# First-layer edits in a two-layer decoder kernel: rotary tables, gate silus, a rotation in PSUM, weight centring

## The chip, the cores and the metric

The kernel runs on one core of a Trainium2 chip. The core has five engines that work side by side, each on its own queue of instructions in a fixed order: PE (TensorE, matmuls and transposes), DVE (VectorE), ACT (ScalarE, activation functions), POOL (GpSimd) and SP (SyncE, which here only starts transfers). Data lies in SBUF (on-chip memory of 128 partitions) and in PSUM (eight banks of 128 x 512 floats, which matmuls write). An engine waits at an instruction until the semaphores of what it needs are set. The metric is device time in microseconds (us), the median of several executions.

## The reference

Two decoder layers work on x of 4 batches x 256 tokens x 256 columns, all in float32. Each layer adds three terms:

```python
x = x + attn(layernorm(x))
x = x + mamba(ctx_1024, layernorm(x))
x = x + ffn(layernorm(x))
```

The first attention has 8 query heads and 2 key heads of 32 columns, a window of 64 tokens, tanh-capped scores and a normalisation behind the rotation. The second has 16 query heads and 4 key heads of 128 columns, with a layer norm of each head ahead of the rotation:

```python
q = _layernorm(q, qn_g, qn_b)
k = _layernorm(k, kn_g, kn_b)
q = q * cos + _rotate_half(q) * sin
k = k * cos + _rotate_half(k) * sin
```

The middle term is a state-space scan over the tokens of ctx_1024, gated by the normalised x:

```python
state = state * dA + (d * u)[..., None] * b[:, None, :]
y = jnp.einsum('bdn,bn->bd', state, c)
...
y = y + D[None, :, None] * x
y = y * silu(z)
```

Here z is the layer norm of the decoder's x. The first feed-forward is a gated one of 704 columns, the second a mixture of 32 experts with a shared one.

## The kernel before

The code is written with a tile framework: it is traced in program order, and the framework then fixes each engine's order itself from its own estimate of times, with code that stands earlier preferred, and sets all waits. A tile of a pool and a tag takes one of that tag's `bufs` buffers. So an engine's order in the trace isn't the order of the code: code that stands far behind fills gaps where its inputs are ready.

The program order is this. `conv_taps(0)` and `mamba_front(0, 0)` prepare the scan of batches 0 and 1 (`s00`). For each batch b, `head0(b)` projects, rotates and normalises queries, keys and values, and `tail0(b)` does scores, softmax, values and output; between them some steps of a scan are run. `head0` works in two halves of 128 tokens (c): the projection `pq` is in the only bank of pool `pa`; L359 multiplies 320 columns by the cosines into `r`, L360 the halves-swapped columns by the sines into `rr`, L365 (ACT) copies the values, and once both halves are there, L368 adds `rr` to `r`. The scan of batches 2 and 3 (`s01`) begins during batch 0.

A scan state (one of 16 per channel half) is an exponential on ACT (L215), a product on POOL (L217), the scan itself on DVE (L218), a product with C on DVE (L220), and a sum: on PE into a bank (L235) for even states, on POOL into y (L237) for odd ones; L239 adds the bank to y at the end of a half.

Behind the first attention, the constants and rows of the second layer (`cst1`, `row`) are asked for on ACT's queue (L513, L514). Then the weights of the second attention are centred, so that each head's projected vector has mean zero: one reduction over all 20 heads (L518), a scaling (L519), and one subtraction on POOL for each of two row blocks (L521).

The first feed-forward runs over two halves of two batches (`hf`). For each batch, `mamba_gate` takes layer-norm statistics of x (`ln_stats`: L120 and L121 on DVE, four small POOL steps L124 to L127), makes `sz` = silu of the normalised x on ACT (L252, two buffers), multiplies y by it (L256), transposes the product (L258) and adds it to x (L264); `ln_transposed` then takes statistics again, normalises (L136), transposes (L140) and copies the result out (L143). Both use the single bank of pool `pc`. Then the matmuls L551, the silu of the gate L559, the product L562 and the down-projection L575, which L583 adds to x. In the second half, `run(s01)` stands ahead of the gates: all that is left of that scan.

Then the pools of the first layer are closed and those of the second attention (`a1w`, `a1`, and eight PSUM banks anew) opened in their room. Seven POOL instructions for queries and seven for keys make the rotary tables (`cg`, `sg`, `bt`, L608 to L617) from `cst1` and `row`. Two transposes of the first `bt` (L626) give `btT` (L627). `keys_values(0)` follows: layer norm, projection (L640), squares (L655, ACT), rotation with the tables (L660 to L668, the product with `cg` in place in PSUM), scaling (L632, L633, L693). The second layer's scan, the attention and the experts (L941 to L955) fill the rest.

Of the kernel before, what the change touches and what calls it, by code (L numbers as in the profile page):

```python
# [10 lines left out]
F32 = mybir.dt.float32  # L11
BF16 = mybir.dt.bfloat16
I32 = mybir.dt.int32
AF = mybir.ActivationFunctionType
# [3 lines left out]
P = 128  # L18
# [23 lines left out]
def decoder_kernel(  # L42
# [203 lines left out]
    def mamba_gate(l, b, pool):  # L246

        nb, rs = ln_stats([x[:, 2 * b + c, :] for c in range(2)])
        pt = ps(pool)
        for c in range(2):  # L250
            sz = work.tile([P, S], F32, tag="sz", name="sz")
            nc.scalar.activation(  # L252
                sz, x[:, 2 * b + c, :], AF.Silu, bias=nb[:, c : c + 1], scale=rs[:, c : c + 1]
            )
            yg = work.tile([P, S], F32, tag="yg", name="yg")
            nc.vector.tensor_mul(yg, y_of[l, b // 2][:, c, (b % 2) * S : (b % 2 + 1) * S], sz)  # L256
            for lh in range(2):
                nc.tensor.transpose(  # L258
                    pt[:, lh * 256 + c * P : lh * 256 + (c + 1) * P],
                    yg[:, lh * P : (lh + 1) * P],  # L260
                    ident,
                )
        xb = x[:, 2 * b : 2 * b + 2, :]
        nc.vector.tensor_add(xb, xb, pt.rearrange("p (t d) -> p t d", t=2))  # L264
# [47 lines left out]
    with ExitStack() as ph:  # L312
# [27 lines left out]
        def head0(b):  # L340
# [5 lines left out]
            for c in range(2):  # L346
# [12 lines left out]
                nc.vector.tensor_mul(r[:, c, 0:10, :], q3, cos.unsqueeze(1).to_broadcast([P, 10, 32]))  # L359
# [4 lines left out]
                )  # L364
                nc.scalar.copy(  # L365
                    r[:, c, 10:12, :], pq[:, 320:384].rearrange("p (h d) -> p h d", d=32)
                )
            nc.vector.tensor_add(r[:, :, 0:10, :], r[:, :, 0:10, :], rr)  # L368
# [146 lines left out]

    wh = wqkv1[:, :, 0 : 20 * D1].rearrange("p f (h d) -> p f h d", d=D1)
    wmean = cpool.tile([P, 2, 20], F32, name="wmean")
    nc.vector.tensor_reduce(wmean, wh, AX.X, ALU.add)  # L518
    nc.vector.tensor_scalar(wmean, wmean, 1.0 / D1, None, ALU.mult)  # L519
    for f in range(2):  # L520
        nc.gpsimd.tensor_sub(wh[:, f], wh[:, f], wmean[:, f, :].unsqueeze(2).to_broadcast([P, 20, D1]))  # L521

    with ExitStack() as ph:
# [14 lines left out]
        for hf in range(2):  # L538
            if hf == 1:
                run(s01)  # L540
            xnT = wp.tile([P, 2, 512], F32, tag="f_xnT", name="f_xnT")
            for bb in range(2):
                mamba_gate(0, 2 * hf + bb, pc)
# [45 lines left out]
    with ExitStack() as ph:  # L589
# [7 lines left out]

        tabs = []
        for gcol, bcol in ((R_QG, R_QB), (R_KG, R_KB)):
            g_ = row[:, gcol - R_BR : gcol - R_BR + D1]  # L600
            b_ = row[:, bcol - R_BR : bcol - R_BR + D1]
            cg = wp.tile([P, 2, D1], F32, name=f"cg{gcol}")
            sg = wp.tile([P, 2, D1], F32, name=f"sg{gcol}")
            bt = wp.tile([P, 2, D1], F32, name=f"bt{gcol}")
            bs = wp.tile([P, 2, D1], F32, name=f"bs{gcol}")
            cos = cst1[:, 0:256].rearrange("p (c d) -> p c d", c=2)
            sin = cst1[:, C_SIN1 - C_COS1 : C_SIN1 - C_COS1 + 256].rearrange("p (c d) -> p c d", c=2)
            nc.gpsimd.tensor_mul(cg, cos, g_.unsqueeze(1).to_broadcast([P, 2, D1]))  # L608
            nc.gpsimd.tensor_mul(bt, cos, b_.unsqueeze(1).to_broadcast([P, 2, D1]))
            for lo, hi in ((0, 64), (64, 0)):  # L610
                for dst, v in ((sg, g_), (bs, b_)):
                    nc.gpsimd.tensor_mul(
                        dst[:, :, lo : lo + 64],
                        sin[:, :, lo : lo + 64],
                        v[:, hi : hi + 64].unsqueeze(1).to_broadcast([P, 2, 64]),
                    )
            nc.gpsimd.tensor_add(bt, bt, bs)  # L617
            tabs.append((cg, sg, bt))
# [535 lines left out]
```

## Time and profile before

| what | value |
|---|---|
| runs | 927.5, 925.39, 924.55 us; median 925.39 |
| profiled execution | 922.39 us, of which the span of instructions is 920.6 |
| mean granted PE clock | 0.931 |
| busy PE / DVE / ACT / POOL | 830.1 / 587.9 / 481.1 / 421.3 us (90, 64, 52, 46%) |
| chain that ended last, by engine | PE 42%, DVE 13%, ACT 7%, POOL 5%, issue 3% |
| first layer (0 to 324 us) | two scans, attention, feed-forward |
| second attention and its scan | 324 to 670 us |
| experts, first and second half | from 673 us to the end |

The page's second part cuts the span into 40 slices of 23 us; each digit is the busy share in tenths, PEclk the granted clock in tenths:

```profile
PE   4999899998978969789988979997999999999997
DVE  3697968666875549879678965867346676312221
ACT  2647635467949626757775765677624343211111
POOL 3263767657774643756673754233337761000000
PEclk9978758897997989999989999998999999999999
```

The first 14 slices are the first layer. No engine is full in all of them, and the clock falls in some of them below full. In the last six slices POOL has nothing, DVE and ACT little, and PE is full. The chain of waits and the timelines of this part are shown with the prediction.

### The profile page before, as it was taken

To read this page: it belongs to the slowest core of one execution; us is meant where nothing else is said; L and a number is where in the kernel's file an instruction comes from. 1 tells how busy PE (TensorE), PEld (TensorE's weight loads), DVE (VectorE), ACT (ScalarE), POOL (GpSimd) and SP (SyncE) were. 2 spreads that over 40 slices of the span, in tenths; PEclk is the share of its full clock that TensorE was granted. 3 is DMA by queue.
4 is the path that set the end of the run, shared out by engine and by line. 5 is a ranking of instruction groups with operands and counts; after the bars stand their busy time and mean duration, and the time that the engine had idled before them with its cause. 6 is when DMAs were issued, how large, how long until landed. Compare 5 with 4: busy or idle time off the path is not lost.

```text
span 920.6 us, 10256 instructions
## 1 busy us (share of the span) xinstructions
PE 830.1 (90%) x3074; PEld 517.2 (56%) x3074; DVE 587.9 (64%) x1096; ACT 481.1 (52%) x1187; POOL 421.3 (46%) x421
## 2 busy tenths in 40 slices
PE   4999899998978969789988979997999999999997
PEld 2455566643443425555664656674666666666665
DVE  3697968666875549879678965867346676312221
ACT  2647635467949626757775765677624343211111
POOL 3263767657774643756673754233337761000000
PEclk9978758897997989999989999998999999999999
DMA  4364436654541220111010200000137743554542
GB/s 158 101 188 168 140 119 183 202 183 165 179 166 51 68 92 1 58 35 46 24 68 6 79 33 23 24 1 2 48 92 234 232 152 102 163 149 146 160 152 80
DMA packets 60999, 98.36 MB, mean 107 GB/s; under 512 B 6336, under 2 KB 26704, under 8 KB 60688
## 3 DMA queue, kind: packets, MB, share of 16 engines
q1 hardware_dynamic: 59232, 95.77, 32.8%
q10 hardware_dynamic: 1712, 1.94, 0.7%
q8 instruction: 24, 0.39, 0.2%
q14 instruction: 31, 0.25, 0.1%
HBM read 96.24 MB, written 1.44 MB: 106 GB/s over the span
## 4 chain that ended last, share of the span: by engine, by line
PE 42%; DVE 13%; ACT 7%; POOL 5%; issue 3%; DMA 0%; SPq 0%; POOLq 0%; ACTq 0%; DVEq 0%
PE ps L941 12%; PE ps L955 12%; PE ps L809 5%; PE ps L640 3%; PE ps L747 2%; PE ps L794 2%; DVE h L218 2%; DVE ps L667 2%; ACT sc L766 2%; DVE qs L660 1%; DVE qr L668 1%; PE ps L674 1%; ACT L215 1%; POOL sc L771 1%; DVE hc L220 1%
## 5 line engine op out<-in xcount | busy, mean ns | idle before, releaser
L217 POOL TENSOR_TENSOR db<-bt,du 128x512 f32<-128x512 f32 x128 | 162.1, 1277 | 100.2 <-DVE h L218 67.9
L218 DVE TENSOR_TENSOR_SCAN h<-h,db 128x512 f32<-128x512 f32 x128 | 152.7, 1217 | 23.4 <-ACT h L215 22.0
L941 PE MATMUL ps<-moe_xnT,w 128*128 128x512 f32 x272 | 129.3, 598 | 0.0
L955 PE MATMUL ps<-w,hT 128*128 128x256 f32 x544 | 128.5, 379 | 0.0
L955 PEld LDWEIGHTS ps<-w,hT 128*128 128x128 f32 x544 | 103.0, 190 | 40.2 <-issue 29.4
L946 DVE SCALAR_TENSOR_TENSOR hT<-ps,gr 128x512 f32<-128x512 f32 x64 | 44.1, 689 | 127.0 <-PE ps L941 127.0
L215 ACT ACTIVATE h<-dt,negA 128x512 f32<-128x512 f32 x128 | 86.4, 689 | 59.2 <-DVE hc L220 58.5
L947 ACT ACTIVATE hT<-hT 128x512 f32<-128x512 f32 x68 | 42.8, 629 | 133.7 <-DVE hT L946 133.6
L640 PE MATMUL ps<-wqkv,xnT 128*128 128x512 f32 x192 | 94.8, 606 | 8.0 <-DVE rq L632 5.7
L220 DVE TENSOR_TENSOR hc<-h,ct 128x512 f32<-128x512 f32 x128 | 85.2, 679 | 3.4 <-DMA ct<-bc 0.9
L227 POOL TENSOR_TENSOR y<-y,hc 128x512 f32<-128x512 f32 x64 | 80.7, 1270 | 8.8 <-DVE hc L220 8.6
L633 POOL TENSOR_TENSOR rq<-rq,nhalf 128x8 f32<-128x8 f32 x20 | 32.9, 1647 | 90.2 <-DVE rq L632 90.0
L941 PEld LDWEIGHTS ps<-moe_xnT,w 128*128 128x128 f32 x272 | 51.7, 191 | 36.5 <-issue 33.2
L655 ACT ACTIVATE sq<-ps 128x128 f32<-128x128 f32 x160 | 42.3, 281 | 40.7 <-PE ps L640 37.5
L766 ACT ACTIVATE sc<-sc,nm 128x256 f32<-128x256 f32 (+1 forms) x128 | 56.7, 448 | 12.6 <-DVE nm L761 8.6
L771 POOL TENSOR_TENSOR sc<-sc,rsum 128x512 f32<-128x512 f32 (+1 forms) x32 | 46.2, 1466 | 34.5 <-DVE rsum L769 33.6
L809 PE MATMUL ps<-wo,oT 128*128 128x256 f32 x256 | 57.0, 381 | 0.4 <-ACT oT L802 0.4
L809 PEld LDWEIGHTS ps<-wo,oT 128*128 128x128 f32 x256 | 48.1, 190 | 9.2 <-ACT oT L802 2.6
L640 PEld LDWEIGHTS ps<-wqkv,xnT 128*128 128x128 f32 x192 | 33.5, 194 | 30.1 <-issue 17.7
L674 PE MATMUL ps<-ident,qr 128*128 128x128 f32 x160 | 28.4, 295 | 19.6 <-DVE qr L668 17.6
L235 PE MATMUL ps<-hc,ident 128*128 128x512 f32 x64 | 39.8, 712 | 5.5 <-DVE hc L220 5.3
L237 POOL TENSOR_TENSOR y<-y,hc 128x512 f32<-128x512 f32 x32 | 41.1, 1283 | 7.3 <-DVE hc L220 5.0
(205 smaller groups left out, 1505.5 us busy)
## 6 DMA issues: line engine op xcount, KB each, us to landing
bt<-bc SPq DMA_DIRECT2D x96, 256.0 KB, 3.6
ct<-bc SPq DMA_DIRECT2D x96, 256.0 KB, 3.7
w<-in_w_dram SPq DMA_DIRECT2D x64, 256.0 KB, 3.5
gr<-gt SPq DMA_DIRECT2D x64, 256.0 KB, 3.5
wqkv<-in_wqkv_dram SPq DMA_DIRECT2D x1, 3072.0 KB
wo<-in_wo_dram SPq DMA_DIRECT2D x1, 2048.0 KB, 8.6
x<-in_x_dram SPq DMA_DIRECT2D x4, 256.0 KB, 5.1
w<-in_ws_dram SPq DMA_DIRECT2D x4, 256.0 KB, 3.3
```

What stands on the lines that cost most here:

```text
L215: nc.scalar.activation(h, dt[:, c, :], AF.Exp, scale=negA[:, a : a + 1])
L217: nc.gpsimd.tensor_mul(db, bt, du[:, c, :])
L218: nc.vector.tensor_tensor_scan(h, h, db, 0.0, ALU.mult, ALU.add)
L220: nc.vector.tensor_mul(hc, h, ct)
L227: nc.gpsimd.tensor_add(y[:, c, :], y[:, c, :], state(n, c, bt, ct))
L640: mm(pq, lhsT=xnT[:, f, c * P : (c + 1) * P], rhs=wqkv1[:, f, ch * 512 : (ch + 1) * 512], start=(f == 0), stop=(f == 1),)
L766: nc.scalar.activation(part, part, AF.Exp, bias=nm[:, qc, j : j + 1], accum_out=rsum[:, qc, j : j + 1])
L771: nc.gpsimd.tensor_mul(part, part, rsum[:, qc, :].unsqueeze(2).to_broadcast([P, 4, w]))
L809: mm(pout[:, c * 256 : (c + 1) * 256], lhsT=oTs[h // 4][:, h % 4, c * P : (c + 1) * P], rhs=wo1[:, 8 * gp + h, :], start=(h == 0), stop=(h ...
L941: mm(ph_, lhsT=w[:, f * P : (f + 1) * P], rhs=xnT[:, f, :], start=(f == 0), stop=(f == 1))
L946: gated.append(nc.vector.scalar_tensor_tensor(h, ph_, 0.0, g, ALU.max, ALU.mult).ins)
L955: mm(po[t // 2][:, (t % 2) * 256 : (t % 2 + 1) * 256], lhsT=h[:, t * P : (t + 1) * P], rhs=w[:, 256:512], start=start and t % 2 == 0, stop ...
```

## The change

Four edits, all in the first layer's part of the program.

- The rotary tables of the second attention are made ahead of the weight centring, in a pool that lives through the whole kernel; the buffer `bs` is shared by both tables.
- A new function `gates_of` holds a gate's statistics and its two silus; `mamba_gate` takes its result, or calls it. In the first layer the gates of both batches of a half are asked for at the top of the half, in four buffers, for the second half ahead of `run(s01)`. In the second layer the gate is as before, save that both silus stand ahead of the first product.
- In `head0` the sines' product comes first, the cosines' product is written back to PSUM in place, and the sum is made for each half of 128 tokens, from PSUM and `rr`.
- The weight centring is cut into four pieces of five heads.

```diff
--- before.py
+++ after.py
@@ -243,17 +243,24 @@
             if next(gen, "end") == "end":
                 break
 
-    def mamba_gate(l, b, pool):
+    def gates_of(b, pool, bufs):
 
         nb, rs = ln_stats([x[:, 2 * b + c, :] for c in range(2)])
+        szs = []
+        for c in range(2):
+            szs.append(pool.tile([P, S], F32, tag="sz", name="sz", bufs=bufs))
+            nc.scalar.activation(
+                szs[c], x[:, 2 * b + c, :], AF.Silu, bias=nb[:, c : c + 1], scale=rs[:, c : c + 1]
+            )
+        return szs
+
+    def mamba_gate(l, b, pool, szs=None):
+
+        szs = szs or gates_of(b, work, 2)
         pt = ps(pool)
         for c in range(2):
-            sz = work.tile([P, S], F32, tag="sz", name="sz")
-            nc.scalar.activation(
-                sz, x[:, 2 * b + c, :], AF.Silu, bias=nb[:, c : c + 1], scale=rs[:, c : c + 1]
-            )
             yg = work.tile([P, S], F32, tag="yg", name="yg")
-            nc.vector.tensor_mul(yg, y_of[l, b // 2][:, c, (b % 2) * S : (b % 2 + 1) * S], sz)
+            nc.vector.tensor_mul(yg, y_of[l, b // 2][:, c, (b % 2) * S : (b % 2 + 1) * S], szs[c])
             for lh in range(2):
                 nc.tensor.transpose(
                     pt[:, lh * 256 + c * P : lh * 256 + (c + 1) * P],
@@ -356,16 +363,17 @@
                 cos = cst[:, C_COS0 + 32 * c : C_COS0 + 32 * c + 32]
                 sin = cst[:, C_SIN0 + 32 * c : C_SIN0 + 32 * c + 32]
                 q3 = pq[:, 0:320].rearrange("p (h d) -> p h d", d=32)
-                nc.vector.tensor_mul(r[:, c, 0:10, :], q3, cos.unsqueeze(1).to_broadcast([P, 10, 32]))
                 nc.vector.tensor_mul(
                     rr[:, c].rearrange("p h (two d) -> p h two d", two=2),
                     pq[:, 0:320].rearrange("p (h two d) -> p h two d", two=2, d=16)[:, :, ::-1, :],
                     sin.rearrange("p (two d) -> p two d", two=2).unsqueeze(1).to_broadcast([P, 10, 2, 16]),
                 )
+
+                nc.vector.tensor_mul(q3, q3, cos.unsqueeze(1).to_broadcast([P, 10, 32]))
+                nc.vector.tensor_add(r[:, c, 0:10, :], q3, rr[:, c])
                 nc.scalar.copy(
                     r[:, c, 10:12, :], pq[:, 320:384].rearrange("p (h d) -> p h d", d=32)
                 )
-            nc.vector.tensor_add(r[:, :, 0:10, :], r[:, :, 0:10, :], rr)
 
             rf = r.rearrange("p c h d -> p (c h) d")
             mean = small.tile([P, 24], F32, tag="a0_mean", name="a0_mean")
@@ -513,12 +521,38 @@
     nc.scalar.dma_start(out=cst1, in_=consts[:, C_COS1:C_COLS])
     nc.scalar.dma_start(out=row, in_=rows[:, R_BR:R_COLS].to_broadcast([P, R_COLS - R_BR]))
 
+    tabs = []
+    for gcol, bcol in ((R_QG, R_QB), (R_KG, R_KB)):
+        g_ = row[:, gcol - R_BR : gcol - R_BR + D1]
+        b_ = row[:, bcol - R_BR : bcol - R_BR + D1]
+        cg = cpool.tile([P, 2, D1], F32, name=f"cg{gcol}")
+        sg = cpool.tile([P, 2, D1], F32, name=f"sg{gcol}")
+        bt = cpool.tile([P, 2, D1], F32, name=f"bt{gcol}")
+        bs = cpool.tile([P, 2, D1], F32, tag="bs", name="bs")
+        cos = cst1[:, 0:256].rearrange("p (c d) -> p c d", c=2)
+        sin = cst1[:, C_SIN1 - C_COS1 : C_SIN1 - C_COS1 + 256].rearrange("p (c d) -> p c d", c=2)
+        nc.gpsimd.tensor_mul(cg, cos, g_.unsqueeze(1).to_broadcast([P, 2, D1]))
+        nc.gpsimd.tensor_mul(bt, cos, b_.unsqueeze(1).to_broadcast([P, 2, D1]))
+        for lo, hi in ((0, 64), (64, 0)):
+            for dst, v in ((sg, g_), (bs, b_)):
+                nc.gpsimd.tensor_mul(
+                    dst[:, :, lo : lo + 64],
+                    sin[:, :, lo : lo + 64],
+                    v[:, hi : hi + 64].unsqueeze(1).to_broadcast([P, 2, 64]),
+                )
+        nc.gpsimd.tensor_add(bt, bt, bs)
+        tabs.append((cg, sg, bt))
+
     wh = wqkv1[:, :, 0 : 20 * D1].rearrange("p f (h d) -> p f h d", d=D1)
     wmean = cpool.tile([P, 2, 20], F32, name="wmean")
-    nc.vector.tensor_reduce(wmean, wh, AX.X, ALU.add)
-    nc.vector.tensor_scalar(wmean, wmean, 1.0 / D1, None, ALU.mult)
-    for f in range(2):
-        nc.gpsimd.tensor_sub(wh[:, f], wh[:, f], wmean[:, f, :].unsqueeze(2).to_broadcast([P, 20, D1]))
+    for h in range(0, 20, 5):
+        hs = slice(h, h + 5)
+        nc.vector.tensor_reduce(wmean[:, :, hs], wh[:, :, hs], AX.X, ALU.add)
+        nc.vector.tensor_scalar(wmean[:, :, hs], wmean[:, :, hs], 1.0 / D1, None, ALU.mult)
+        for f in range(2):
+            nc.gpsimd.tensor_sub(
+                wh[:, f, hs], wh[:, f, hs], wmean[:, f, hs].unsqueeze(2).to_broadcast([P, 5, D1])
+            )
 
     with ExitStack() as ph:
         wp = ph.enter_context(tc.tile_pool(name="f0w", bufs=1))
@@ -536,11 +570,12 @@
         conv_taps(1)
         scans = []
         for hf in range(2):
+            szs = [gates_of(2 * hf + bb, fp, 4) for bb in range(2)]
             if hf == 1:
                 run(s01)
             xnT = wp.tile([P, 2, 512], F32, tag="f_xnT", name="f_xnT")
             for bb in range(2):
-                mamba_gate(0, 2 * hf + bb, pc)
+                mamba_gate(0, 2 * hf + bb, pc, szs[bb])
                 ln_transposed(2 * hf + bb, xnT[:, :, bb * S : (bb + 1) * S], pc)
             hT = wp.tile([P, NIC, 512], F32, tag="hT", name="hT")
             for ic in range(NIC):
@@ -594,28 +629,6 @@
         wo1 = wp.tile([P, NH1, HID], F32, name="wo1")
         nc.sync.dma_start(out=wo1, in_=wo1_in)
 
-
-        tabs = []
-        for gcol, bcol in ((R_QG, R_QB), (R_KG, R_KB)):
-            g_ = row[:, gcol - R_BR : gcol - R_BR + D1]
-            b_ = row[:, bcol - R_BR : bcol - R_BR + D1]
-            cg = wp.tile([P, 2, D1], F32, name=f"cg{gcol}")
-            sg = wp.tile([P, 2, D1], F32, name=f"sg{gcol}")
-            bt = wp.tile([P, 2, D1], F32, name=f"bt{gcol}")
-            bs = wp.tile([P, 2, D1], F32, name=f"bs{gcol}")
-            cos = cst1[:, 0:256].rearrange("p (c d) -> p c d", c=2)
-            sin = cst1[:, C_SIN1 - C_COS1 : C_SIN1 - C_COS1 + 256].rearrange("p (c d) -> p c d", c=2)
-            nc.gpsimd.tensor_mul(cg, cos, g_.unsqueeze(1).to_broadcast([P, 2, D1]))
-            nc.gpsimd.tensor_mul(bt, cos, b_.unsqueeze(1).to_broadcast([P, 2, D1]))
-            for lo, hi in ((0, 64), (64, 0)):
-                for dst, v in ((sg, g_), (bs, b_)):
-                    nc.gpsimd.tensor_mul(
-                        dst[:, :, lo : lo + 64],
-                        sin[:, :, lo : lo + 64],
-                        v[:, hi : hi + 64].unsqueeze(1).to_broadcast([P, 2, 64]),
-                    )
-            nc.gpsimd.tensor_add(bt, bt, bs)
-            tabs.append((cg, sg, bt))
         mask1 = cst1[:, C_MASK1 - C_COS1 : C_MASK1 - C_COS1 + 384]
         qks = 1.0 / math.sqrt(D1)
```

## The prediction

> **What bounds the kernel.** I read first the chain of waits (the work that ended last, followed back from the end), in order of time. From 670 to 749 us and again from 773 us it is almost nothing but PE lines of the expert layer, back to back; PE is 90% busy over the span. The edits all lie before 335 us, where the chain changes engine every microsecond, so I read that part closely. Columns: start, duration, engine, tile, line.
>
> ```profile
> 323.98 0.73 POOL cg L608
> ...
> 327.71 0.69 POOL bt L617
> 328.40 0.04 issue
> 328.45 0.69 PE ps L626 x2
> 329.14 0.44 PE ps L140 x2
> ...
> 330.17 0.57 ACT xnT L143
> ...
> 331.24 3.21 issue
> 334.45 1.15 ACT sq L655 x8
> ```
>
> PE ends the first layer's feed-forward at 323.85. Then GpSimd makes the first rotary table, two transposes (L626) wait for it, and behind them on PE stand the transposes (L140) of the normalised x. The first square (L655) starts at 334.45: 10.6 us in which PE does 0.69 + 0.44 us of work and one projection.
>
> Second, the same chain where the gate meets the feed-forward of the second half:
>
> ```profile
> 272.20 0.09 DVE ln_mv L121
> ...
> 275.63 1.09 ACT sz L252 x2
> 276.72 0.48 ACT f_xnT L143
> 277.20 0.04 issue
> 277.25 1.13 PE ps L258 x4
> ```
>
> The silus of batch 3's gate (L252), whose x was final at 197 us, stand in the chain. Their statistics come directly behind the previous layer norm's, here and at 201.9 us: the small tiles are handed out in the order of the code.
>
> Third, the timelines of DVE and of POOL at the weight centring:
>
> ```profile
> 95.07 5.47 DVE L518 TENSOR_REDUCE wmean<-wqkv 128x40 f32<-128x5120 f32 x1
> 104.25 4.71 DVE L368 TENSOR_TENSOR r<-r,rr 128x640 f32<-128x640 f32 x1
> ```
> ```profile
> 103.81 4.47 POOL L521 TENSOR_TENSOR wqkv<-wqkv,wmean 128x2560 f32<-128x2560 f32 x1
> ```
>
> One reduction holds DVE for 5.47 us. The addition L368, 0.83 us when alone at 25.8, lasts 4.71 us beside the subtraction L521. Two scan states that ended at 93.7 get their product (L220) only at 101.1, and the next scans start at 108.9.
>
> Fourth, busy time by stretch (stretch, its length, busy us of PE, PEld, DVE, ACT, POOL, granted clock, DMA share, GB/s):
>
> ```profile
> 109.00:142.00 33.00, 31.37 (x100) 20.99 (x100) 23.00 (x36) 10.43 (x23) 20.96 (x15) 0.50 0.38 122
> 143.00:176.00 33.00, 32.94 (x190) 23.21 (x188) 28.56 (x41) 19.34 (x46) 25.42 (x22) 1.00 0.66 197
> 328.40:334.00 5.60, 4.75 (x10) 2.66 (x11) 0.43 (x1) 1.57 (x3) 4.32 (x10) 0.50 0.38 159
> ```
>
> PE is full in the first two, with the same attention code; at a clock of 0.50 it issues 100 matmuls, at 1.00 it issues 190. After the table wait the clock is 0.50 too.
>
> **The sum**, against the profiled execution (922.39 us, span 920.6 and 1.8 around it; the median of the runs is 925.39, 3.0 more).
>
> 1. Tables. 14 GpSimd instructions, 7.3 us from 323.98 to 332.0 less 0.7 of layer-norm work between, leave this place. Least gain: the stall alone, 328.45 - 323.85 = 4.6 us. Most: if L626, L140 and the copy L143 are done before 323.85, the first projection starts there. Four such matmuls take 1.73 us at full clock (row at 399.3), so squares start at 325.6 instead of 334.45: 8.9 us. The room is there: PSUM of the new pools is used early already (the exponentials of the second layer's scan write theirs at 287.2), the xn for L140 are ready at 285.9, and PE waits 1.58 us for DVE before 316.16. If the transposes stay behind 323.85 and only the clock is kept, 3.66 us of projection (330.79 to 334.45) become 1.73: 4.6 + 1.9 = 6.5. I take **7.5**, between the last two. Late next: the projections, and the squares behind them on ACT.
>
> 2. The tables' new place. They need the constants and rows asked for on ACT's queue at 8.8 and 14.0 us. The cover is POOL's idle 14.4 to 33.7 us (19.3 us). With constants landing 3.8 us after issue (median) at least 13 us remain for 7.3. I take 0; without that cover up to 7.3, for POOL is 13.9 to 17.3 of 23 us busy in most later slices. No DMA moves.
>
> 3. Second half's gate (batch 3). Out of the chain: its statistics between the two aggregations (0.39) and its silus ahead of the copy f_xnT: L140 ends at 275.56, the copy starts at 276.72, 1.16. Gain **1.5**. At least 0, if the scan ends later; at most 3, if batch 3's transposes were also to pass batch 2's layer norm.
>
> 4. First half's gate (batch 1). A table load (205.16) and two silus delay f_xnT from 205.6 to 206.96 and the products yg to 208.06; the x addition at 210.01 can come at 207.35, 2.7 us earlier, as can the first matmul of the feed-forward (223.18). The half is closed by the end of the scan (y at 268.66), which shares the engines with the feed-forward, so I count half: **1.3** (0 to 2.7).
>
> 5. The silus' place on ACT. Eight silus as before. Layer 0 has five table loads for them now (95.4, 101.5, 205.2, 220.1, 233.1), at 1.28 us each, each paid again on the way back. After it can be two (silus side by side) or eight: -7.7 to +7.7 us on ACT. Between 143 and 176 ACT is 19.3 of 33 us busy and waits for PE; from 220 to 256 it is full. I take 0. The gates' POOL steps (1.6 us each) and statistics (0.8) pass ahead of the scan's last part: the same work earlier.
>
> 6. Centring and rotation. DVE: four reductions of 5.47/4 = 1.37 us and four small ones of 0.17 for 5.47 + 0.67, the same. POOL: eight of 4.47/4 = 1.12, the same, with six starts more of some 0.05. The longest block falls from 5.47 to 1.37. Rotation: four additions L368, 0.83 + 1.28 + 1.36 + 4.71 = 8.2 us, become eight of 320 columns with one operand in PSUM. The nearest row is L360, 0.478: 3.8 us. The product in place is L359 again. Gain on DVE 4.3. That such an addition does not stretch beside POOL is borne out by L220 (PSUM and SBUF in): 128 times between 0.647 and 0.693. The projection's bank is held 0.48 us longer, eight times; the copy L365 on ACT comes that much later, hidden while PE has the other batch. DVE is busy 141 of 184 us from 92 to 276, so not all of it counts. I take **2.0**; ends -2 (a worse order of queues) and 7.4 (the whole hold of L220).
>
> Sum: 7.5 + 1.5 + 1.3 + 2.0 = 12.3, so 910.1 profiled, and with the 3.0 a median of **913**. It passes on one to one: behind 335 us every step is tied to the one before, PE has no gap from 670 to 749, and the second scan, which ends at 759.8 in the chain, is issued step by step with that work.
>
> A rule against item 2: the Trainium skill, "SBUF — State Buffer", section "SBUF: two separate sides", says that a GpSimd operation and a VectorE operation with two SBUF inputs lock each other out for a whole instruction. The 4.71 us of L368 agrees. By it the 14 table products, now made under a working DVE, could hold DVE by up to their 7.3 us, and the sum would be 5.0 instead of 12.3.
>
> **Rivals.**
>
> *The stall is only half won* (transposes behind 323.85, a cold clock, nothing gained before 268 us): 4.6 + 1.5 = 6.1, 919.3. For it: the new pools' SBUF opened only at 323.9. Against it: PSUM and xn are free before. Chance 0.19.
>
> *The cold spell of 109 to 142 us goes.* It begins after PE was busy only 3.0 of 4 us (104 to 108), in the very place where DVE and POOL were blocked. Its 33 us of full PE at half clock cost up to 16.5; half passed on is 8: 905. Against it: other low clocks (176 to 188, 0.57) stand where no such block is. Chance 0.15.
>
> *Slower: the cold spell gets longer.* The shifted order lets the clock stay at 0.50 over the next batch's attention too (143 to 176, PE 32.94 of 33 us busy, now at 1.00). Every us of that work costs one more, and the scan's exponentials stand behind the tanh rows on ACT. It decides from 12.3 + 2.8 = 15.1 us of work on. With 20 hit it is 925.4 - 12.3 + 20 = 933. For it: the spell outlived 30 us of full PE. Against it: the edits shorten blocks. Chance 0.09.
>
> *Nothing: another wait takes the place* of the tables (DVE's x at 323.88, its layer norm, or a scan that ends later by item 5): 925. Chance 0.05.
>
> A rule here: the Trainium skill, "TensorE: Matmul & The Clock Gate", Part 1, says that some 3.4 us of sustained matmuls release the clock. The trace differs: 31.37 of 33 us busy at 0.50. By the rule, the second and third rival could not exist and 913 would stand; by the trace they keep their chances.
>
> **Numbers.** Forecast 913, chance 0.52, own range 906 to 919. The range 900 to 925 takes in the first two rivals and leaves out the slower one and the whole of both gains at once. A measurement of this kernel tells about 0.3% (2.8 us) from no change. Faster by more: 0.52 + 0.15 + 0.17 (of the half-won case 0.02 falls inside) = 0.84. Same: 0.07. Slower: 0.09.
>
> **What would show it.** Tables on POOL before 40 us; first square no later than 327 us less what was won before; clock 1.00 there. No silu between the last scan and f_xnT of the second half; y of the last scan some 3 us before 268.7. The rotation's additions at about 0.48 us each, no DVE row of 4 us near 100. It is wrong if stretches between 90 and 200 us show a clock of 0.50 for longer than 45 us in all, if ACT has more than eight table loads for layer 0's silus, or if PE waits 4 us or more behind the last down-projection.

## The result, and the profile after

| | before | after |
|---|---|---|
| median of the runs | 926.44 us (924.55 to 928.71) | 914.14 us (911.45 to 916.6) |
| ratio to before | | 0.988, 95% interval 0.9843 to 0.9916 |
| profiled execution / its span | 922.39 / 920.6 us | 916.6 / 914.8 us |
| mean granted PE clock | 0.931 | 0.937 |
| last y of the first layer's scan (L239) | 268.66 | 272.40 |
| last x of the first feed-forward | 323.88 | 327.12 |
| first square of the second attention | 334.45 | 330.00 |
| from there to the end of the span | 586.15 | 584.8 |

The kernel is faster, by 1.2%; 914.14 lies beside the forecast of 913. The two profiled executions are only 5.8 us apart: the one of after is the slowest of its runs, the one of before is 4 us below its median. Executions of one kernel scattered by up to 2.7% in the sessions below (before from 908 to 932 us, one execution of 2815 us aside), and the comparison leaves out those over 1.5% above a kernel's fastest, so a ratio of runs can differ from the ratio of the two medians.

The slices of after, to be read against those of before (same 40 cuts of the span):

```profile
PE   4999899988976979889898979997999999999997
...
DVE  4797998456885569879669875867256776221221
ACT  2748563368747926757766664676523343211111
POOL 5474758455685624747665653333337661000000
PEclk9979797588996999999989999998999999999999
```

In the slices the clock is the row to read: from 115 to 138 us (sixth digit) it goes from 5 to 9, from 161 to 184 (eighth) from 8 to 5, and at the seam (322 to 345, fifteenth) from 8 to 9. The landmarks say what came of it. The first layer's scan ends 3.7 us *later* than before; the way from there to the last x of the feed-forward takes 54.72 instead of 55.22; then 2.88 us instead of 10.57 to the first square. -3.74 + 0.50 + 7.69 = 4.45 us sooner, and 1.35 more behind it.

The seam of the two layers, in the chain of waits of after (start, duration, engine, tile, line; L610 was L575, L618 was L583, L653 was L640, L668 was L655):

```profile
316.59 3.69 PE ps L610 x14
...
321.05 6.05 PE ps L610 x24
327.10 0.02 issue
327.12 0.70 DVE x L618
327.82 0.14 issue
327.96 1.97 PE ps L653 x4
...
330.00 1.15 ACT sq L668 x8
```

After the last addition of the feed-forward (DVE x, L618) the projections start within 0.14 us. There is no POOL row and no transpose between them, and four projection matmuls take 1.97 us where before 3.66 passed up to the first square: the clock did not fall (1.00 from 327 to 333, before 0.52). The tables are now made here, on POOL's timeline (the last bracket is POOL's idle time before the row and what ended it):

```profile
17.28 0.73 POOL L534 TENSOR_TENSOR cg<-cst,row 128x256 f32<-128x256 f32 x1 [2.96 <-DMA row<-in_rows_dram]
17.97 0.73 POOL L535 TENSOR_TENSOR bt<-cst,row 128x256 f32<-128x256 f32 x1
...
25.12 0.73 POOL L543 TENSOR_TENSOR bt<-bt,bs 128x256 f32<-128x256 f32 x1
```

The gate of the second half, in the chain of waits of after (L263 was L256, L265 was L258, L271 was L264):

```profile
272.40 0.70 DVE y L239
...
277.68 1.09 ACT xn L136 x2
...
278.79 1.28 ACT L190
...
280.08 0.70 ACT dt L190
...
280.82 2.07 PE ps L188 x2
282.89 1.06 PE ps L265 x4
...
283.98 0.69 DVE x L271
```

The silu is gone from the chain, as the change intends. In its place stand a table load and the softplus of the second layer's scan (L190), and on PE that scan's matmuls (L188), which go ahead of the gate's transposes (L265). From y to the second x addition it is 11.58 us; before it was 9.74.

Weight centring and rotation, on DVE's timeline of after:

```profile
89.59 1.48 DVE L550 TENSOR_REDUCE wmean<-wqkv 128x10 f32<-128x1280 f32 x1
...
95.78 0.47 DVE L366 TENSOR_TENSOR rr<-ps,cst 128x320 f32<-128x320 f32 x1
...
97.31 0.47 DVE L372 TENSOR_TENSOR ps<-ps,cst 128x320 f32<-128x320 f32 x1
...
98.28 0.47 DVE L373 TENSOR_TENSOR r<-ps,rr 128x320 f32<-128x320 f32 x1
...
105.86 0.69 DVE L239 TENSOR_TENSOR y<-y,ps 128x512 f32<-128x512 f32 x1 [1.55 <-POOL y L237]
```

One reduction of 5.47 us became four of about 1.47 (L550), the additions (L373) take 0.439 to 0.492 us, eight times, and none is stretched. The first half of `s00` ends at 105.86 (before 117.12), all of `s00` at 156.41 (before 166.90). So the parts did locally what they say; yet the first half of `s01` ends at 235.23 (before 228.43). Where that went, in busy time by stretch (columns as with the prediction), first after, then before:

```profile
100.00:140.00 40.00, 38.58 (x202) 25.11 (x200) 36.48 (x55) 21.74 (x54) 28.34 (x25) 0.97 0.57 168
140.00:190.00 50.00, 49.84 (x186) 34.02 (x185) 30.66 (x46) 17.74 (x43) 30.11 (x28) 0.62 0.39 121
190.00:240.00 50.00, 42.19 (x108) 18.38 (x106) 32.42 (x54) 43.17 (x55) 28.43 (x34) 0.93 0.44 153
```

```profile
100.00:140.00 40.00, 37.40 (x131) 24.77 (x131) 30.00 (x43) 18.66 (x42) 25.59 (x17) 0.61 0.35 110
140.00:190.00 50.00, 49.94 (x253) 34.89 (x252) 36.61 (x54) 26.75 (x60) 31.96 (x27) 0.87 0.59 179
190.00:240.00 50.00, 43.11 (x108) 18.10 (x107) 38.53 (x59) 38.37 (x48) 34.34 (x39) 0.90 0.54 186
```

Before, PE was cold in 100 to 140 and issued 131 matmuls; after, 202 at 0.97. Then it turns round: 253 before, 186 after, at 0.62 and with PE 49.84 of 50 us busy. Over both stretches that is 384 matmuls before and 388 after. The scan shows the same: counting the scans (L218) done, after leads with 27 to 22 at 140 us and with 34 to 30 at 160, and is behind with 37 to 38 at 180 and 42 to 43 at 200. The cold spell was not removed; it moved behind, and by its end the lead of four to five scans was gone.

What after loses beyond that, it loses at a clock that is no lower. From 190 to 240 us both kernels issue 108 matmuls, at 0.93 after and 0.90 before, but DVE is busy 32.42 us instead of 38.53. On DVE's timeline of after two waits stand there (the bracket is DVE's idle time before the row and what ended it):

```profile
205.62 0.69 DVE L271 TENSOR_TENSOR x<-x,ps 128x512 f32<-128x512 f32 x1 [5.51 <-PE ps L265]
...
218.18 0.75 DVE L597 SCALAR_TENSOR_TENSOR hT<-ps,par,sg 128x512 f32<-128x512 f32 x1 [5.09 <-PE ps L586]
```

The first is the gate's addition to x, waiting for the gate's transposes, the second the first product of the feed-forward. Before, no wait of DVE in this stretch is longer than 2.4 us. no_tabs has the same two waits (5.5 and 5.3 us) and its last y at 271.98. So the second loss looks like one of the order of the queues, not of the clock.

### The profile page after: what moved, and what is told of

The parts are those of the page before. It is cut to its first block, busy times and chain, and to the rows that moved or that the text cites. A ratio compares the mean times of both kernels' runs of the same rounds, so it can differ in the third digit from the quotient of the medians.

```text
span 914.8 us, 10269 instructions
## 1 busy us (share of the span) xinstructions
PE 823.8 (90%) x3074; PEld 513.6 (56%) x3074; DVE 585.3 (64%) x1106; ACT 475.4 (52%) x1182; POOL 423.1 (46%) x427
## 4 chain that ended last, share of the span: by engine, by line
PE 43%; DVE 13%; ACT 7%; POOL 4%; issue 3%; DMA 0%; SPq 0%; POOLq 0%; ACTq 0%; DVEq 0%
PE ps L954 12%; PE ps L968 12%; PE ps L822 5%; PE ps L653 3%; PE ps L760 2%; PE ps L807 2%; DVE ps L680 2%; ACT sc L779 2%; DVE qs L673 1%; DVE qr L681 1%; DVE h L218 1%; PE ps L687 1%; PE ps L610 1%; ACT sq L668 1%; POOL sc L784 1%
## 5 line engine op out<-in xcount | busy, mean ns | idle before, releaser
L217 POOL TENSOR_TENSOR db<-bt,du 128x512 f32<-128x512 f32 x128 | 162.0, 1278 | 95.9 <-DVE h L218 63.8
L218 DVE TENSOR_TENSOR_SCAN h<-h,db 128x512 f32<-128x512 f32 x128 | 152.3, 1215 | 14.7 <-ACT h L215 14.6
L653 PE MATMUL ps<-wqkv,xnT 128*128 128x512 f32 x192 | 93.2, 597 | 8.0 <-DVE rq L645 5.6
L668 ACT ACTIVATE sq<-ps 128x128 f32<-128x128 f32 x160 | 42.5, 282 | 48.2 <-PE ps L653 48.2
L235 PE MATMUL ps<-hc,ident 128*128 128x512 f32 x64 | 40.9, 733 | 11.1 <-DVE hc L220 10.7
L653 PEld LDWEIGHTS ps<-wqkv,xnT 128*128 128x128 f32 x192 | 32.9, 190 | 29.2 <-issue 18.0
```

What stands on the lines that cost most here:

```text
L217: nc.gpsimd.tensor_mul(db, bt, du[:, c, :])
L218: nc.vector.tensor_tensor_scan(h, h, db, 0.0, ALU.mult, ALU.add)
L653: mm(pq, lhsT=xnT[:, f, c * P : (c + 1) * P], rhs=wqkv1[:, f, ch * 512 : (ch + 1) * 512], start=(f == 0), stop=(f == 1),)
L668: nc.scalar.activation(sq, pq[:, i * D1 : (i + 1) * D1], AF.Square, accum_out=ss[:, i : i + 1])
```

## The experiments

Each kernel was run beside the kernel before in its session. Landmarks come from one profiled execution each. In five rows the ratio and the ratio of the two medians differ by more than the interval: r_only (1.0028 and 0.9950), rot_tabs (1.0012 and 0.9924), no_gates (1.0213 and 1.0061), no_cent (1.0170 and 1.0008) and all_front (0.9988 and 0.9857). There the comparison with before is open.

| kernel | median (before's there) | ratio, 95% interval | last y | last x to first square | first square | from there to end |
|---|---|---|---|---|---|---|
| t_only: tables alone | 915.64 (924.73) | 0.9892, 0.9849 to 0.9935 | 271.18 | 2.83 | 329.96 | 586.2 |
| g_only: silus alone | 935.78 (924.73) | 1.0138, 1.0072 to 1.0204 | 279.79 | 10.78 | 345.67 | 588.1 |
| r_only: rotation alone | 920.08 (924.73) | 1.0028, 0.9975 to 1.0082 | 260.98 | 10.78 | 327.23 | 588.2 |
| c_only: centring alone | 944.52 (924.73) | 1.0192, 1.011 to 1.0273 | 294.26 | 10.78 | 358.77 | 587.1 |
| rot_tabs: rotation, tables | 916.38 (923.36) | 1.0012, 0.9971 to 1.0053 | 268.29 | 2.83 | 328.54 | 586.8 |
| no_tabs: all but tables | 924.15 (923.36) | 1.0035, 0.9993 to 1.0077 | 271.98 | 10.46 | 336.65 | 587.4 |
| no_gates: all but silus | 931.86 (926.2) | 1.0213, 1.01 to 1.0326 | 283.05 | 2.87 | 340.15 | 584.8 |
| no_cent: all but centring | 926.96 (926.2) | 1.017, 1.0037 to 1.0303 | 279.18 | 2.82 | 336.70 | 584.8 |
| cent_warm | 943.33 (923.36) | 1.0212, 1.0133 to 1.0291 | 288.83 | 10.46 | 352.85 | 587.4 |
| all_warm | 942.08 (923.36) | none | 287.31 | 2.88 | 345.73 | 585.3 |
| all_front | 912.92 (926.2) | 0.9988, 0.9905 to 1.007 | 268.65 | 2.83 | 327.12 | 583.8 |
| tabs_front | 918.13 (924.66) | 0.994, 0.9894 to 0.9986 | 254.30 | 6.42 | 313.86 | 596.9 |

### One part alone

Each of the four takes one part of the diff shown above and leaves the rest as before. t_only has the table block behind the constants' requests and not behind the first layer; g_only has `gates_of` and its two calls. The other two:

```diff
 r_only
-                nc.vector.tensor_mul(r[:, c, 0:10, :], q3, cos.unsqueeze(1).to_broadcast([P, 10, 32]))
...
+                nc.vector.tensor_mul(q3, q3, cos.unsqueeze(1).to_broadcast([P, 10, 32]))
+                nc.vector.tensor_add(r[:, c, 0:10, :], q3, rr[:, c])
...
-            nc.vector.tensor_add(r[:, :, 0:10, :], r[:, :, 0:10, :], rr)
 c_only
-    nc.vector.tensor_reduce(wmean, wh, AX.X, ALU.add)
+    for h in range(0, 20, 5):
+        hs = slice(h, h + 5)
+        nc.vector.tensor_reduce(wmean[:, :, hs], wh[:, :, hs], AX.X, ALU.add)
...
```

> Only the rotary tables move. The sum's theory: 7.5 us less than before (ratio 0.992), the first square (L655 before) near 327 us, the last scan's y where it was (268.7 us within 1). The rival, that the tables carry the whole change and the other three edits cancel each other: 11 to 12 us less (ratio 0.987 to 0.988). The rival of a half-won stall: 4.6 us less (0.995) and a granted clock of 0.50 behind the down-projection.

> Only the gates' silus move. The sum's theory: 2.8 us less (ratio 0.997): 1.3 before the last scan's y (268.7 to 267.4) and 1.5 between it and the first matmul of the second feed-forward half. The rival, seen in the changed kernel's trace where that y came at 272.4: the silus cost ACT table loads in front of the scan, the y comes 2 to 4 us later than 268.7, and the time is equal or up to 3 us more (1.000 to 1.003).

> Only the rotation in PSUM. The sum's theory: the four additions of 8.2 us on DVE become eight of 0.48, some 1 us of it shows (ratio 0.999). The rival: the bank held longer, or another static order, delays the first attention: the last scan's y later than 268.7 by 2 us or more, ratio 1.002 to 1.006. A third: the cold clock spell from 109 to 142 us goes with the 4.7 us addition, 5 to 8 us less (0.992 to 0.995).

> Only the centring in four pieces. The sum's theory: DVE's block of 5.47 us becomes four of 1.4, some 1 us shows (ratio 0.999). The rival: with eight GpSimd subtractions spread out, each holds DVE's instructions with two SBUF inputs, and the last scan's y comes 2 to 4 us later than 268.7 (1.002 to 1.004). A third: the cold spell goes, 5 to 8 us less (0.992 to 0.995).

Measured: the tables alone give all of the gain that can be told (0.9892; all four parts 0.988). The silus alone and the centring alone make it 1.4% and 1.9% slower, the rotation alone can't be told from no change. The medians of the four stand 9, 5 us below and 11, 20 us above before; added, that would be a kernel some 17 us slower, and the four together are 12 us faster. The last y says why the parts can't be added: it goes from 261 to 294 us by edits that touch a few microseconds of work each. The profiled execution of c_only is its slowest (947.73, median 944.52), so its 294 is used for the direction alone.

### Two and three parts

rot_tabs and no_tabs, no_gates, no_cent are made of the same pieces: each of the last three is the changed kernel with one part put back, as here the centring of no_cent, against after:

```diff
-    for h in range(0, 20, 5):
...
+    nc.vector.tensor_reduce(wmean, wh, AX.X, ALU.add)
+    nc.vector.tensor_scalar(wmean, wmean, 1.0 / D1, None, ALU.mult)
+    for f in range(2):
+        nc.gpsimd.tensor_sub(wh[:, f], wh[:, f], wmean[:, f, :].unsqueeze(2).to_broadcast([P, 20, D1]))
```

> Tables moved and rotation in PSUM, silus and centring as before. If the parts add: the tables' 7.7 us between the last addition to x and the first square, and the rotation's 0 to 5, so 8 to 13 us less than before (ratio 0.986 to 0.992) and as fast as the changed kernel or faster. If each new order draws its cold spells afresh in the first attention: the 7.7 us stay in their place, but the last scan's y comes anywhere from 260 to 280 us and the ratio lies between 0.98 and 1.01.

> The changed kernel with the tables back in their old place. If the parts add as they were measured alone (silus +1.4%, rotation +0.3%, centring +1.9%): 1.03 or more of the kernel before. If they do not add, and the three of them together are about neutral as the changed kernel says (its gain is little more than the tables'): 0.995 to 1.005, with 10.6 us from the last addition to the first square.

> Tables, rotation and centring changed, silus as before. If the centring costs its 1.9% in any company: 7.7 us for the tables against 18 for the centring, 1.010 or more of before. If its cost alone was an accident of that one order: 0.985 to 0.995. The silu of batch 3 is back in the chain, and batch 3's addition to x comes 9.7 us behind the last scan's y, as in the kernel before, where the changed kernel has 11.6.

> Tables, rotation and silus changed, centring in one piece. If the silus cost their 1.4% in any company: 1.000 to 1.010. If the four edits' effects ahead of the last scan depend on the order that they give together: anywhere from 0.985 to 1.005, with 2.8 to 2.9 us from the last addition to x to the first square all the same.

Measured: without the tables the other three parts together are worth nothing that can be told (1.0035, interval to 0.9993 below). With the tables, but without the silus or without the centring, the gain is gone: medians of 931.86 and 926.96, 18 and 13 us above after's and 6 and 1 us above before's beside them. Whether these two are slower than before is open: the ratios say 2%, the medians 0.6 and 0.1%. So the silus and the centring each cost alone, and neither can be taken out of the changed kernel by itself: no sign can be given to either. rot_tabs leaves out both and has a median of 916.38, which can't be told from after's 914.14 or from t_only's 915.64; its ratio to before is undecided.

The price of the tables in their old place hardly depends on the other edits. PE's timeline of no_tabs at the seam (the bracket is PE's idle time before the row and what ended it):

```profile
330.77 0.44 PE L639 MATMUL ps<-ident,bt 128*128 128x128 f32 x2 [4.61 <-POOL bt L630]
331.05 0.94 PE L140 MATMUL ps<-ident,xn 128*128 128x128 f32 x4
332.78 5.41 PE L653 MATMUL ps<-wqkv,xnT 128*128 128x512 f32 x6 [0.79 <-ACT xnT L143]
```

The transposes of the table wait 4.61 us for POOL, the copy of xnT takes 0.79 more, and the projections stand in 5.41 us for six. Every kernel with the tables in the old place takes 10.46 to 10.78 us from the last x to the first square; all but one with them in the new place take 2.82 to 2.88.

### Is it the cold clock?

cent_warm is c_only, all_warm the changed kernel, each with the idle matmuls that precede the scores raised from two to five (their results are overwritten, nothing else differs):

```diff
-                    for _ in range(2):
+                    for _ in range(5):
                         mm(psc[:, 0:320], lhsT=identb, rhs=far, start=True, stop=True)
```

> Centring in pieces alone, and five idle matmuls (far by identb, overwritten) in place of two ahead of each head's scores in the first attention, so that PE has more columns in flight there. Nothing of the result changes. If the 1.9% that the centring cost alone is the half clock of 112 to 150 us: the half-clock time ahead of 344 us falls from 133 us to under 90, and the ratio to 0.99 to 1.005. If it is the blocked queues: the half clock may fall, but the time stays at 1.015 or more.

> The changed kernel with five idle matmuls in place of two ahead of each head's scores. Nothing of the result changes. If the clock of the first attention sets how late its scans end: half-clock time falls from 92 us to under 60 and the time to 0.975 to 0.985 of before. If PE's added work (96 matmuls of 0.15 to 0.24 us, 14 to 23 us) costs more than the clock gives: 0.99 to 1.005.

Measured: from 0 to 344 us the mean granted clock is 0.81 in c_only, 0.87 in cent_warm and 0.85 before. Yet cent_warm stays near c_only: its median is 943.33 beside 944.52, its last y comes at 288.83 instead of 294.26. all_warm has no higher clock than after (0.87 both), and all of its runs (932.74 to 949.99) lie above all of after's (911.45 to 916.6).

Neither kernel changes the clock alone, however. Busy time of the idle matmuls, and of nothing else, up to 300 us, in c_only and then in cent_warm (stretch, length, busy us of PE and PEld, granted clock, DMA share, GB/s):

```profile
0.00:300.00 300.00, 18.59 (x64) 5.30 (x64) 0.80 0.47 150
```
```profile
0.00:300.00 300.00, 35.30 (x160) 16.69 (x160) 0.87 0.48 150
```

The 96 further matmuls take 16.7 us more of PE ahead of the scores. In all_warm it is 17.6 us more than in after (34.10 instead of 16.48), and there the last y comes 14.9 us later. What the warming can have won is of the same size. Counted in slices of 2 us, each weighted with twice its missing share of the clock, the time at half clock up to the last y is 116 us in c_only, 72 in cent_warm and 78 before. PE issued 190 matmuls in 33 us at full clock and 100 at half, so 44 us less of half clock are worth up to some 22 us (an estimate). Less the 16.7, that leaves 5; the last y came 5.4 sooner. So these two kernels do not decide: a cold clock that costs its full price fits them as well as one that costs nothing. Busy time by stretch of c_only, then of cent_warm:

```profile
140.00:190.00 50.00, 49.04 (x212) 33.45 (x212) 36.87 (x53) 21.40 (x52) 33.82 (x29) 0.74 0.43 132
190.00:240.00 50.00, 43.62 (x132) 23.74 (x132) 28.29 (x46) 28.73 (x42) 25.56 (x33) 0.70 0.45 148
```

```profile
140.00:190.00 50.00, 46.37 (x263) 33.02 (x262) 37.31 (x54) 21.86 (x53) 31.05 (x26) 0.94 0.57 169
190.00:240.00 50.00, 43.05 (x120) 20.85 (x120) 26.59 (x43) 31.38 (x42) 23.69 (x31) 0.76 0.38 123
```

In 140 to 190 cent_warm has 0.94 and 263 matmuls against 212 of c_only, but 70 and 27 of them are the idle ones, which leaves 193 against 185. In 190 to 240 DVE is busy only 28.29 and 26.59 of 50 us in the two (before 38.53), with PE at 43 to 44 and POOL at 24 to 26 of 50.

The traces on record say a little more. In the profiled executions (of c_only its slowest) c_only spends 37.5 us more at half clock than before and its last y comes 25.6 us later, so by the same estimate the clock can account for up to 19 of them. Over the twelve kernels without added matmuls the last y goes with the time at half clock ahead of it, from 61 us and 254.30 in tabs_front to 116 us and 294.26 in c_only (correlation 0.93). That does not show which causes which. For the changed kernel the clock's sum explains nothing: 75 us at half clock up to the last y, before 78, and the y is 3.7 us later.

### The second layer's front in another place

The softplus that took the silus' place belongs to `mamba_front(1, 0)`, the preparation of the second layer's scan, which stands at the end of the first feed-forward half. Here it is asked for only behind the gates of the second half (all_front against after; tabs_front is t_only with the same move):

```diff
                 ln_transposed(2 * hf + bb, xnT[:, :, bb * S : (bb + 1) * S], pc)
+            if hf == 1:
+                scans.append(mamba_front(1, 0, pf))
...
-            scans.append(mamba_front(1, hf, pf))
+            if hf == 1:
+                scans.append(mamba_front(1, 1, pf))
```

> The changed kernel with the second layer's front of batches 0 and 1 (projection, softplus, products) placed in program order behind the gates of the second half. Theory: the changed kernel loses its scan's lead between 160 and 230 us because this front's table loads and matmuls fill ACT and PE there, and loses 1.8 us at batch 3's gate to its softplus. Then the last scan's y comes 4 us or more before 272.4, batch 3's addition to x 9 to 10 us behind it instead of 11.6, and the time falls to 0.975 to 0.985 of before. Rival: that work only moves and meets the second half's silus, or the second layer's scan starts late: 0.988 to 1.00.

> Only the tables moved, and the second layer's front of batches 0 and 1 put behind the gates of the second half; silus, rotation and centring as before. If the front is what takes the lead of the scan between 160 and 230 us in any order: the last scan's y comes ahead of the 271.2 of the tables alone by 3 us or more, and the median is 908 to 913. If the place of the front helps only with the other three edits: y at 268 to 275, median 914 to 920, as with the tables alone. 2.8 to 2.9 us from the last addition to x to the first square in both.

Measured: in all_front y to x is 8.79 us (268.65 to 277.44) instead of 11.58, so the softplus and its matmuls were what held the gate up, and the last y comes 3.75 us sooner than in after. The median of all_front is 912.92, the one of after 914.14 in another session: within the scatter, and its ratio is open. tabs_front, where the silus stay in their old place, takes 12.60 us from y to x. It has the earliest last y of all, 254.30, but its execution ends at 912.59 and its median at 918.13: of 16.1 us won against t_only at the first square, 10.7 are given back behind it. Of the second layer's scans, t_only has done eight by 319 us, beside the feed-forward; tabs_front starts the first at 313.5 and ends the eighth at 348. Part of the front's work also stands at the seam, on PE's timeline of tabs_front:

```profile
307.33 1.12 PE L188 MATMUL ps<-xdbl,dtproj 8*128 8x512 f32 x2
308.38 0.44 PE L630 MATMUL ps<-ident,bt 128*128 128x128 f32 x2
308.66 0.60 PE L140 MATMUL ps<-ident,xn 128*128 128x128 f32 x4
309.23 1.12 PE L188 MATMUL ps<-xdbl,dtproj 8*128 8x512 f32 x2
310.28 4.97 PE L644 MATMUL ps<-wqkv,xnT 128*128 128x512 f32 x7
```

Matmuls of the front (L188) stand ahead of the table's transposes (L630) and between the transposes of x (L140) and the projections (L644): the one kernel where moved tables leave 6.42 us. No version that was run beats the changed kernel by what can be told.

## Why the prediction was right, and where not

The forecast of faster by some 12 us was right, and for one reason, the first term. Of the other three terms none came as summed; that the median lies 1 us from the forecast all the same is in part luck. By its own steps:

**1. Tables, 7.5: right in size and mechanism.** 7.69 us between the last x and the first square. Of these, 4.57 are the wait for the tables (323.88 to 328.45). The two pieces on which the choice between 6.5 and 8.9 hung both came true: the transposes of the table (L639, L626 before) are done at 296 us and the copy xnT at 300, and the clock stays at 1.00. 0.84 us of the possible gain is left: the chain has the projections released by DVE's addition at 327.12, though their own inputs had long been there. The rival *half won* (6.1) fell with this.

**2. Tables' new place, 0: right.** They run from 17.3 to 25.8 us in POOL's idle time, and t_only keeps its whole 7.74 us at the seam. The DVE operation that stretched most beside them is the product `diag` (L304, L297 before): 1.22 us before, 1.69 after, 1.41 in t_only. The Trainium skill, "SBUF — State Buffer", section "SBUF: two separate sides", would have charged up to 7.3 us of DVE for them; the trace shows 0.47 us, for few operations of DVE there read two SBUF tiles.

**3. Second half's gate, 1.5: not realised.** The silus left the chain as the step says, but batch 3's addition to x comes 1.84 us later behind y (9.74 to 11.58). From y to the last x of the feed-forward it is 0.5 us less (55.22 to 54.72), which can't be put down to the gate: no_gates, with the silus in their old place, has 54.23, and all_front, with y to x at 8.79, has 55.64. What failed is the count of what is late next: the step took the copy f_xnT as next in line. In the gap ACT took a table load and a softplus of the second layer, 2.0 us, and PE its 2.07 us of matmuls. g_only, no_cent and no_tabs have the same order and 11.56 or 11.57 us from y to x; with the front moved it is 8.79. Moving the silus saved 0.95 us there (9.74 to 8.79), the softplus and its matmuls took 2.79.

**4. First half's gate, 1.3: not realised.** From the attention's last x to batch 1's gate it was 13.50, after 13.31. The two silus no longer stand ahead of f_xnT. But batch 0's two, made at 96.7 and 102.8 us before, now run with batch 1's behind the attention, and POOL takes a scan product ahead of the statistics. From the timeline of all engines of after:

```profile
192.72 2.06 ACT L252 ACTIVATE sz<-x,ln_nb,ln_rs 128x256 f32<-128x256 f32 x4
...
196.46 0.67 DVE L271 TENSOR_TENSOR x<-x,ps 128x512 f32<-128x512 f32 x1
...
199.24 0.15 DVE L121 BATCH_NORM_AGGREGATE ln_mv<-ln_st 128x2 f32<-128x6 f32 x1
...
199.46 1.27 POOL L217 TENSOR_TENSOR db<-bt,du 128x512 f32<-128x512 f32 x1 [4.14 <-issue]
...
200.82 0.22 POOL L124 TENSOR_SCALAR ln_nb<-ln_mv 128x2 f32<-128x2 f32 x1
```

The statistics of batch 0 are ready at 199.4, with a scan of DVE between their two aggregations, and wait until 200.82 for L217; x to the first of them is 4.36 us, before 2.49.

**5. The silus on ACT, 0: right.** One table load of their own (212.85) instead of five; the four of the first half share that of u (L173). That gave no visible time, as assumed.

**6. Centring and rotation, 2.0: the step that failed.** The local costs held (four additions of 8.2 us in all became eight of under 0.5 each; POOL's eight subtractions took 1.25 to 1.70 instead of 1.12 us, about 0.18 us for a further start where the step had 0.05). What did not follow is the sum from DVE's freed time to the end of the scan: the first half of `s00` came 11.3 us earlier and the last y 3.7 us later, where steps 4 and 6 together said 3.3 earlier. The two rivals on the clock show what lies between. *The cold spell of 109 to 142 us goes* came true (0.97 there), and so did the mechanism of *the cold spell gets longer*, in the place it named, the next batch's attention (0.62 in 140 to 190). They cancelled: from 90 to 200 us, counted in slices as above, both kernels spend 47.8 us at half clock. That is over the 45 us given as a sign of being wrong, but before had no less. The Trainium skill, "TensorE: Matmul & The Clock Gate", Part 1, has some 3.4 us of sustained matmuls release the clock; 49.84 of 50 us busy at 0.62 disagree, if busy in the profile is what the page means. That the moved cold spell took the lead up to 190 us, and DVE's two waits of 5.51 and 5.09 us the rest, is the reading of the traces; no run isolates either, so how much of the 7 us is clock and how much queue order stays open. The sum of the cold time is no longer than before (75 and 78 us up to the last y).

**Passing on one to one: right.** From the first square to the end it is 583.8 to 588.2 us in thirteen kernels (before and after among them), while the first square moves by 32 us. The exception is tabs_front, which pushes scans of the second layer behind that point.

So of the 12.3 us summed, the seam's 7.7 are shown; the rest was predicted at 4.8 and is -3.2 in the profiled execution up to the first square. Two of the signs that the prediction named did not come: the first square is at 330.00, not by 327, and the last y is 3.7 us later, not 3 sooner. That the medians are also 12.3 apart owes something to scatter, which is wider than the 0.3% that the prediction allowed: the profiled pair has 5.8, and t_only, which has the first term alone, 9.

Left open: what holds the scan up between 160 and 290 us where the centring, or the silus, stand alone, and what share of it is the clock's. To fix the engines' order by hand in both kernels would settle it; that was not tried.

## What to carry to other kernels

Work that stands alone on the seam between two stages, with PE waiting and the clock falling, was worth its full time here when moved into an engine's idle time, and could be summed from rows. In the stretch where five queues are interleaved by a planner, the gain of a part could not be summed, and not even its sign alone held in company: read the landmarks (last scan, first matmul of the next stage) of the whole, and test parts together. A kernel that warms the clock by added work tests the added work too: subtract it before the clock is cleared. When an instruction leaves the path that sets the end, look which ready instruction of later code the planner will put in its place; here that took more than was freed.

## What was not expected of the hardware

PE stayed at a clock of 0.62 over 50 us in which it was 49.84 us busy, and five idle matmuls ahead of each score instead of two raised the mean clock of the first 344 us from 0.81 to 0.87 in c_only but not in the changed kernel (0.87 both). A subtraction of 640 columns on POOL took 1.25 us where one of 2560 took 4.47: four cost 0.53 more than one, about 0.18 for each further start. Small DVE operations on SBUF tiles stretched beside POOL, L551 from 0.16 to 1.15 us and yg from 0.41 to 1.50, while the additions with one operand in PSUM never did (0.439 to 0.492).
